# Four transformer layers with attention over a long context: where transposes, maxima and first products stand in the queues

## The chip, the cores and the metric

The kernel runs on one core of one Trainium2 chip. The metric is the device time of one execution in microseconds (us). TensorE (PE) multiplies, VectorE (DVE) reduces and does arithmetic, ScalarE (ACT) evaluates functions and copies, GpSimd (POOL) does small arithmetic and masks, SyncE (SP) issues DMAs. "PEld" is PE's weight load.

## The reference

`x` is 16 batch elements of 256 tokens by 128 channels, `ctx` 16 contexts of 1601 rows by 64 channels. Four layers follow each other, each an attention and a feed-forward part, each added to `x`:

```python
x = x + l0_attn(ln(x), ctx); x = x + l0_ffn(ln(x))   # self attention (causal) + cross attention, heads of 8
x = x + l1_attn(ln(x), ctx); x = x + l1_ffn(ln(x))   # cross attention, heads of 8
x = x + l2_attn(ln(x), ctx); x = x + l2_ffn(ln(x))   # self attention, then cross attention, heads of 32
x = x + l3_attn(ln(x), ctx); x = x + l3_ffn(ln(x))   # cross attention, heads of 8
# every attention: softmax(q k^T * scale) v, 16 heads; cross: k, v from ctx (1601 rows)
# the feed-forward parts: expert layers with top-k routing, and one quantised layer with a convolution
```

All of it is float32; the results are 16 x 256 x 128.

## The kernel before

**Units of work.** The cross attentions make up most of the work. There are 16 elements x 4 layers = 64 of them, and each is cut into four slabs of four heads (of 8 or of 32 channels), so 256 slabs: 192 with heads of 8 (`att.d8`), 64 with heads of 32. Two elements are under way at once (`LANES = 2`), and a list `seq` gives the order: for elements 0 and 1: l0 of both, l1 of both, l2 of both, l3 of both; then elements 2 and 3; eight rounds in all.

**A slab** goes through seven steps over its 13 tiles of 128 keys, two at a time. In a step PE makes transposed scores (`st_ops`, tile `st`), subtracting the maxima by further products with `nmT`; ACT takes the exponential (`exps`, L464, tile `p`); and PE multiplies the probabilities of the step before with the values (`weigh`, called from `weigh_back`), into an accumulator `av`, one bank of PSUM of 512 columns. With heads of 8, the values have a ninth column of ones, so that sums and values come out together (9 rows a head, columns 0 to 255 of the bank). With heads of 32, the values go to columns 0 to 255 (`av[:, 0, :]`) and the sums, products with `ones`, to columns 256 to 511 (`av[:, 1, :]`).

**Accumulators.** Before the first product, `zeroed` writes zeros over the accumulator with one product of a single row of zeros (`zero16`, a part of the tile `rows`): 256 columns for heads of 8, 512 for heads of 32. All other products add (`start` is False).

**Maxima.** While a slab is worked on, the maxima of the next one are prepared: 32 products per slab (`Slab.maxima`, tile `bank`), each reduced by DVE (L552, into `mx`), spread over steps 0 to 5. Then `Slab.thirds` reduces once more on DVE (L558, `nm`), and the helper `thirds` splits each maximum into three bfloat16 parts by four small POOL instructions (L509 to L512, tile `nmp`). Before, this is issued at the start of step 6. After the products of step 6 `Slab.shift` transposes `nmp` on PE, and ACT copies the result (`nmT`).

**The end of a slab.** The last products of a slab are issued in step 0 of the next one. `finish` then runs `normalised` as a generator: for heads of 8, ACT copies the accumulator (`y`, L488 calls the copy at L239), the generator yields, and when it is next advanced PE transposes `y` (L492), and DVE divides by the ninth column (L495, L496). For heads of 32 DVE does it all (L502, L503), without a yield. When the slab was the fourth, `att.done` is set, which lets the element's own chain go on.

**Slots.** All other work (layer norms, projections, feed-forward parts, self attention, loading and projecting the context) is written as generators. A slot (`slot()`) advances one of them after the other by one yield: first the pending `later` (the end of a slab), then one of two lines in turn (`key_line`, `value_line`, which make the keys and values), then each chain in the order of the list `chains`. After the products of each step come two slots, or three when the next entry of `seq` is an l2. The order of all instructions is fixed in this way when the program is built; every engine works off its own queue.

**Self attention** (`own_attention`, in l0 with heads of 8 and in l2 with heads of 32) runs inside slots: maxima for the four slabs (`mx`, L579), thirds, a shift of all four, and then per slot one slab's scores and exponentials, the next older one's sums (l2) and masks on POOL (`affine_select`, L603), and the values of the one before.

**DMAs around the change.** Queries and keys for heads of 8 are split into two parts (`hl`, L401 to L405, four buffers) and spread over partitions by SP (`spread`, L411): 16 DMAs for queries, 16 for an element's own keys, 4 for a slab of context keys. SP also loads the weights of the feed-forward parts (`stream`, L266, tile `ws`; `li` are those behind an l2 attention), which the kernel asks for three slots ahead of the product `down`, and the contexts (`cn`, L352 to L355), whose norms take POOL and DVE instructions over 128 x 832 elements (L361 to L370).

The lines that a generator resumes at are told by its yields. The matmul helper `mm` is L172; tiles tell its groups apart.

Of the kernel before, what the change touches and what calls it, by code (L numbers as in the profile page):

```python
# [20 lines left out]
P = 128  # L21
T = 256
# [52 lines left out]
def model(ctx: ExitStack, tc: tile.TileContext, d, out):  # L75
# [26 lines left out]
    ones = const.tile([P, P], F32, name="ones")  # L102
# [11 lines left out]
    zero16 = rows[0:1, : T // 2].bitcast(BF16)  # L114
# [56 lines left out]
    def mm(o, l, r, start=True, stop=True, free=False):  # L171
        nc.tensor.matmul(out=o, lhsT=l, rhs=r, start=start, stop=stop, skip_group_check=free)  # L172
# [6 lines left out]
    with setup as sp:  # L179
# [40 lines left out]
        for h0, c in ((64, 0), (96, P)):  # L220
            r = rows[h0 : h0 + 1, c : c + P]
# [14 lines left out]
    def evac(o, i, bias=None):  # L236

        if bias is None:
            nc.scalar.copy(o, i)  # L239
        else:  # L240
            nc.scalar.activation(o, i, AF.Identity, bias=bias)
# [222 lines left out]
        nc.scalar.activation(e[:r, :, :n, :], sc[:r, :, :n, :], AF.Exp, scale=att.scale)  # L464
        return e

    def zeroed(att):
        a = bank().rearrange("p (u q) -> p u q", u=2)
        n = 1 if att.d8 else 2
        mm(a[:, :n, :], zero16[:, :P], zero16.unsqueeze(1).broadcast_to([1, n, T]), True, False, True)  # L470
        return a

    def weigh(att, s, av, pr, t0, n, r, last, heads=range(4), sums=True, values=True):
        for i in range(n):
            fin = last and i == n - 1
            if values:
                for g in heads:
                    m = 9 if att.d8 else 32
                    mm(av[32 * g : 32 * g + m, 0, :], att.value(s, t0 + i, g, r), pr[g // 2][:r, g % 2, i, :],
                       False, fin, True)  # L480
            if sums and not att.d8:
                for g in heads:
                    mm(av[32 * g : 32 * g + 32, 1, :], ones[:r, :32], pr[g // 2][:r, g % 2, i, :], False, fin, True)

    def normalised(att, s, av):
        if att.d8:
            y = chan("y8")[:, :T]
            evac(y, av[:, 0, :])  # L488
            yield
            t = bank()  # L490
            for q in range(2):
                nc.tensor.transpose(t[:, q * P : (q + 1) * P], y[:, q * P : (q + 1) * P], ident)  # L492
            tv = t[:, :T].rearrange("p (q g e) -> p q g e", q=2, g=4)
            rc = sm.tile([P, 2, 4], F32, tag="rc8", name=name("rc8"))
            nc.vector.reciprocal(rc, tv[:, :, :, 8])  # L495
            nc.vector.tensor_tensor(  # L496
                att.o[:, :, 32 * s : 32 * s + 32].rearrange("p q (g e) -> p q g e", g=4),
                tv[:, :, :, :8], rc.unsqueeze(3).broadcast_to([P, 2, 4, 8]), ALU.mult,
            )
        else:  # L500
            rc = chan("rc")[:, :T]
            nc.vector.reciprocal(rc, av[:, 1, :])  # L502
            nc.vector.tensor_tensor(att.o[:, s, :], av[:, 0, :], rc, ALU.mult)  # L503
# [23 lines left out]
    class Slab:  # L527


        steps = [(t, min(2, NT - t), rows_of(t)) for t in range(0, NT, 2)]  # L530
# [13 lines left out]
        def maxima(self):  # L544

            g, q, c, k0, k1 = self.todo.popleft()
            att, s = self.att, self.s
            p = bank()
            h = slice(32 * g, 32 * g + 32)

            def reduce():
                nc.vector.tensor_reduce(self.mx[:, q, g, c : c + 1], p[:, : k1 - k0], AX.X, ALU.max)  # L552

            return lambda: mm(p[:, : k1 - k0], att.q[h, s, q * P : (q + 1) * P], att.k[s][h, k0:k1]), reduce
# [9 lines left out]
    def own_attention(att, causal, select):  # L564

        nm = sm.tile([P, 4, 2, 4], F32, tag="nm4", name=name("nm4"), bufs=1)
        for s in range(4):
            sc = [ps.tile([P, 2, 2, T], F32, tag="st", name=name("mx4")) for _ in range(2)]
            for q in range(2):
                for g in range(4):  # L570
                    h = slice(32 * g, 32 * g + 32)
                    mm(sc[g // 2][:, g % 2, q, :], att.q[h, s, q * P : (q + 1) * P], att.k[s][h, :],
                       q == 0, q == 1 and not causal)
            if causal:
                for g in range(4):
                    mm(sc[g // 2][:, g % 2, :, :], ident16, caus, False, True)
            for hp in range(2):
                o = nm[:, s, :, 2 * hp : 2 * hp + 2].rearrange("p q g -> p g q")
                nc.vector.tensor_reduce(o, sc[hp], AX.X, ALU.max, negate=True)  # L579
            yield  # L580
        for s in range(4):
            thirds(nmp[2 + s], nm[:, s, :, :])
            if s % 2:
                yield
        nmT = shift_T([nmp[2 + s] for s in range(4)])
        yield
        op, sign = select
        prs, avs, end = {}, {}, None
        for u in range(6):
            if end is not None:  # L590
                advance(end)
                end = None
            if 2 <= u:
                s = u - 2
                weigh(att, s, avs[s], prs.pop(s), 0, 2, P, True, sums=False)
                end = normalised(att, s, avs.pop(s))
                advance(end)
            if 1 <= u < 5:
                s = u - 1
                avs[s] = zeroed(att)  # L600
                weigh(att, s, avs[s], prs[s], 0, 2, P, True, values=False)
                for e in prs[s]:
                    nc.gpsimd.affine_select(  # L603
                        out=e, in_=e, pattern=[[0, 2], [sign * P, 2], [-sign, T]],
                        compare_op=op, fill=0.0, base=0, channel_multiplier=sign,
                    )
            if u < 4:
                prs[u] = [exps(att, t, 2, P) for t in st_ops(att, u, 0, 2, P, nmT[:, u, :])]
            yield
        advance(end)  # L610
        return att.o


# [442 lines left out]
    def advance(g):  # L1056
        try:
            return True, next(g)
        except StopIteration:
            return False, None  # L1060
# [62 lines left out]
    with tc.manual_schedule():  # L1123
        sl = slab(0)
        while sl.todo:
            for o in sl.maxima():
                o()
        sl.thirds()
        sl.shift()
        back = None  # L1130

        def weigh_back():

            nonlocal back
            if back is None:
                return
            sl, i, j, pr = back
            n = i // 4
            t0, m, r = sl.steps[j]
            if j == 0:  # L1140
                until(lambda: (0 if sl.att.d8 else sl.s) in v_of.get(n, {}))
                sl.att.v = v_of[n]
                sl.av = zeroed(sl.att)
            last = j == len(sl.steps) - 1
            weigh(sl.att, sl.s, sl.av, pr, t0, m, r, last)
            back = None
            if last:
                g = finish(sl, i)
                if advance(g)[0]:
                    later.append(g)  # L1150

        for i in range(4 * len(seq)):
            nxt = slab(i + 1)
            steps = sl.steps
            emitted = 0

            def maxima(want):

                nonlocal emitted
                ops = []  # L1160
                while nxt is not None and emitted < want:
                    a, c = nxt.maxima()
                    a()
                    ops.append(c)
                    emitted += 1
                for c in ops:
                    c()

            for j, (t0, m, r) in enumerate(steps):

                part = 32 * (j + 1) // (len(steps) - 1)
                if j < len(steps) - 1:
                    maxima(part - 3)
                elif nxt is not None:
                    nxt.thirds()
                sc = st_ops(sl.att, sl.s, t0, m, r, sl.nmT)
                pr = [exps(sl.att, t, m, r) for t in sc]
                if j < len(steps) - 1:
                    maxima(part)
                weigh_back()  # L1180
                back = (sl, i, j, pr)
                if j == len(steps) - 1 and nxt is not None:
                    nxt.shift()
                slot()
                slot()

                if i // 4 + 1 < len(seq) and seq[i // 4 + 1][1] == "l2":
                    slot()
            kp_room.give()
            sl = nxt  # L1190
        weigh_back()
        until(lambda: not chains and not later)

# [118 lines left out]
```

## Time and profile before

| | |
|---|---|
| median of 3 runs | 11116.24 us (11102.46 to 11129.85) |
| the profiled execution, its own time | 11069.08 us |
| its span, first to last instruction | 11067.1 us |
| mean granted PE clock | 0.815 |
| the zero product, 256 columns (heads of 8) | x256, 79.8 us busy, mean 312 ns |
| the zero product, 512 columns (heads of 32) | x128, 52.2 us busy, mean 408 ns |
| maxima, DVE (L552) | x8192, 4155.2 us busy, mean 567 ns |
| exponentials, ACT (L464) | x3840, 3500.5 us busy, mean 963 ns |
| thirds, POOL (L509 to L512) | x384 each, 83.6 + 78.9 + 83.6 + 89.2 us busy |
| masks, POOL (L603) | x256, 266.6 us busy, mean 1063 ns |

The profile is one execution. Busy time is the union of an engine's instructions; [...] In a list of waits, `PE bank L492 <- ACT y L239` means that PE, about to write `bank` at L492, was held until ACT had written `y` at L239; the numbers are the total, the count and the longest. In a timeline each row has the start, the length, the engine, the line, the operation and its tiles, and in brackets how long the engine had been idle before and what ended that. "PEclk" is the share of PE's clock that was granted.

### The profile page before, as it was taken

What the parts mean: (1) busy time and instruction counts of PE and PEld (TensorE: products, weight loads), DVE (VectorE), ACT (ScalarE), POOL (GpSimd) and SP (SyncE); (2) the same over time, 40 slices, a digit from 0 to 9 for tenths busy, and PEclk for the clock granted to TensorE, in tenths of its full rate; (3) what the DMA queues carried; (4) which work ended last, traced back from release to release, by engine and by line L of the source; (5) the groups of instructions that cost most, each with busy time, mean ns of one, the idle gap of its engine ahead of it and who ended that gap; (6) DMA issues with size and microseconds to landing.
All of it is one profiled execution on the core that took longest, in us unless ns stands there. A gap on an engine that the chain in (4) does not pass through costs nothing.

```text
span 11067.1 us, 204917 instructions
## 1 busy us (share of the span) xinstructions
PE 9761.1 (88%) x86834; PEld 5294.4 (48%) x86874; DVE 5929.3 (54%) x13070; ACT 4978.5 (45%) x6812; POOL 952.3 (9%) x2283
## 2 busy tenths in 40 slices
PE   6989899897998979889798897998979889898898
PEld 3445444454444544445454454444545445444454
DVE  5545555455554555545455454554555545465455
ACT  3544455444553445434454344543445434454444
POOL 2000100001000010000100001000010000100000
PEclk8779777797878978789777897778977789687898
DMA  2100111001110011100111001110011100111011
GB/s 58 37 7 15 36 45 37 7 16 39 42 37 7 19 38 42 34 7 19 38 44 32 7 19 42 40 32 7 19 38 43 33 7 19 38 44 32 7 24 27
DMA packets 158828, 313.10 MB, mean 28 GB/s; under 512 B 65163, under 2 KB 116275, under 8 KB 157910
## 3 DMA queue, kind: packets, MB, share of 16 engines
q1 hardware_dynamic: 154676, 297.83, 11.7%
q8 instruction: 683, 11.19, 0.4%
q14 instruction: 235, 1.93, 0.1%
q0 software_dynamic: 768, 1.48, 0.0%
q10 hardware_dynamic: 2466, 0.68, 0.0%
HBM read 98.31 MB, written 2.10 MB: 9 GB/s over the span
## 4 chain that ended last, share of the span: by engine, by line
PE 71%; DVE 14%; ACT 5%; issue 4%; POOL 3%; SPq 2%; DMA 1%; another core or an unknown queue 0%; DVEq 0%; POOLq 0%; ACTq 0%
PE bank L172 57%; PE st L172 10%; DVE mx L552 5%; ACT p L464 3%; DVE nm L579 2%; SPq L411 2%; PE mx L172 1%; PE bank L492 1%; POOL p L603 1%; PE bank L298 1%; DVE z L282 1%; POOL rs L278 1%; DVE st L275 1%; DVE hl L405 1%; ACT y L239 1%
## 5 line engine op out<-in xcount | busy, mean ns | idle before, releaser
L552 DVE TENSOR_REDUCE mx<-bank 128x1 f32<-128x400 f32 (+2 forms) x8192 | 4155.2, 567 | 2296.9 <-PE bank L172 2271.8
L464 ACT ACTIVATE p<-st 128x1024 f32<-128x1024 f32 (+1 forms) x3840 | 3500.5, 963 | 3568.3 <-PE st L172 2358.6
L172 PE MATMUL bank<-k,q 32*128 32x400 f32 (+2 forms) x10240 | 3573.1, 557 | 495.3 <-DVE mx L552 261.3
L172 PEld LDWEIGHTS bank<-k,q 32*128 32x128 f32 x10240 | 1600.6, 211 | 1928.7 <-DVE mx L552 1111.4
L172 PE MATMUL bank<-p,v 128*9 128x256 f32 (+3 forms) x27648 | 2412.4, 460 | 12.6 <-POOL p L603 12.6
L172 PE MATMUL st<-q,k 32*128 32x256 f32 (+1 forms) x18176 | 1974.8, 391 | 126.2 <-DVE nm L579 69.2
L172 PEld LDWEIGHTS st<-q,k 32*128 32x128 f32 (+1 forms) x18176 | 1300.8, 210 | 443.7 <-ACT p L464 140.4
L172 PE MATMUL st<-nmT,ones 32*128 32x512 bf16 (+1 forms) x7680 | 1270.1, 435 | 0.0
L172 PEld LDWEIGHTS bank<-p,v 128*9 128x9 f32 (+3 forms) x27648 | 676.3, 104 | 1175.4 <-issue 922.6
L172 PE MATMUL bank<-p,ones 128*32 128x256 f32 (+1 forms) x7680 | 607.1, 389 | 18.1 <-ACT p L464 18.1
L509 POOL CAST nmp<-nm 128x8 bf16<-128x8 f32 x384 | 83.6, 218 | 5441.9 <-DVE nm L558 3668.7
L278 POOL TENSOR_TENSOR rs<-rs,neghalf 128x2 f32<-128x2 f32 x240 | 167.5, 698 | 3491.1 <-DVE rs L277 3491.1
L172 PEld LDWEIGHTS <-ones 32*128 32x128 bf16 (+1 forms) x7680 | 408.1, 108 | 39.4
L579 DVE TENSOR_REDUCE nm<-mx 128x4 f32<-128x1024 f32 x256 | 301.8, 1221 | 215.3 <-PE mx L172 210.6
L239 ACT COPY v<-bank 128x512 f32<-128x512 f32 (+3 forms) x592 | 228.6, 448 | 328.8 <-PE bank L172 328.8
L172 PEld LDWEIGHTS bank<-p,ones 128*32 128x32 f32 (+1 forms) x7680 | 250.8, 113 | 216.6 <-ACT p L464 43.6
L502 DVE RECIPROCAL rc<-bank 128x256 f32<-128x256 f32 x128 | 224.9, 1757 | 193.6 <-PE bank L172 189.3
L603 POOL TENSOR_SCALAR_AFFINE_SELECT p<-p 128x1024 f32<-128x1024 f32 x256 | 266.6, 1063 | 653.3 <-PE bank L172 352.7
L464 ACT ACT_TABLE_LOAD x141 | 180.9, 1283 | 312.9 <-PE st L172 201.9
L172 PE MATMUL bank<-ws,h 128*128 128x128 f32 x1664 | 297.9, 343 | 3.2 <-DVE h L1027 0.8
L768 DVE TENSOR_TENSOR x<-bank,x 128x256 f32<-128x256 f32 x144 | 61.1, 425 | 446.0 <-PE bank L172 446.0
L172 PEld LDWEIGHTS bank<-ws,h 128*128 128x128 f32 x1664 | 267.2, 248 | 39.0 <-DVE mx L552 13.6
(240 smaller groups left out, 7274.4 us busy)
## 6 DMA issues: line engine op xcount, KB each, us to landing
k<-hl SPq DMA_DIRECT2D x768, 200.2 KB, 4.0
q<-hl SPq DMA_DIRECT2D x1024, 32.0 KB, 1.9
ws<-in_s_l_a_li_dram SPq DMA_DIRECT2D x32, 768.0 KB, 4.3
ws<-in_s_l3f_dram SPq DMA_DIRECT2D x32, 768.0 KB, 6.7
ws<-in_s_l0f_dram SPq DMA_DIRECT2D x32, 512.0 KB, 5.6
ws<-in_s_l_a_qkv_dram SPq DMA_DIRECT2D x16, 768.0 KB
k<-hl SPq DMA_DIRECT2D x256, 32.0 KB, 1.9
ws<-in_s_l3f_dram SPq DMA_DIRECT2D x16, 384.0 KB
```

The costliest lines, as they stand in the source:

```text
L172: nc.tensor.matmul(out=o, lhsT=l, rhs=r, start=start, stop=stop, skip_group_check=free)
L239: nc.scalar.copy(o, i)
L275: nc.vector.bn_stats(out=st[:, q, :], in_=src[:, q, :])
L278: nc.gpsimd.tensor_tensor(rs, rs, neghalf[:, 0:2], ALU.pow)
L282: nc.vector.tensor_scalar(z[:, q, :], src[:, q, :], mv[:, q, 0:1], rs[:, q : q + 1], ALU.subtract, ALU.mult)
L298: nc.tensor.transpose(p[:, q * P : (q + 1) * P], z[:, q, :], ident)
L411: nc.sync.dma_start(out=raw(o)[r::4, :], in_=raw(hl[c])[32 * s : 32 * s + 32, :])
L464: nc.scalar.activation(e[:r, :, :n, :], sc[:r, :, :n, :], AF.Exp, scale=att.scale)
L502: nc.vector.reciprocal(rc, av[:, 1, :])
L552: nc.vector.tensor_reduce(self.mx[:, q, g, c : c + 1], p[:, : k1 - k0], AX.X, ALU.max)
L579: nc.vector.tensor_reduce(o, sc[hp], AX.X, ALU.max, negate=True)
L603: nc.gpsimd.affine_select(out=e, in_=e, pattern=[[0, 2], [sign * P, 2], [-sign, T]], compare_op=op, fill=0.0, base=0, channel_multiplier=sign,
```

## The change

Four things are done:

1. `normalised` yields twice, not once, between the copy of `y` and its transposes. In `own_attention` the generator is advanced at the start of the next slot and then driven to its end after that slot's value products; at the end the rest takes a slot of its own.
2. `Slab.thirds` of the next slab is called in step 5, after the last maxima and ahead of `weigh_back` and the slots of that step, not at the start of step 6.
3. `zeroed` becomes `accumulators`: for heads of 32 nothing is written; the first product of each head into the bank has `start` set (the values in the cross attention; the sums in `own_attention`, where they come first and the values `after`). For heads of 8 the zero product stays.
4. The calls follow (`weigh` has a new argument).

```diff
-    def zeroed(att):
+    def accumulators(att):
+
         a = bank().rearrange("p (u q) -> p u q", u=2)
-        n = 1 if att.d8 else 2
-        mm(a[:, :n, :], zero16[:, :P], zero16.unsqueeze(1).broadcast_to([1, n, T]), True, False, True)
+        if att.d8:
+            mm(a[:, 0, :], zero16[:, :P], zero16, True, False, True)
         return a
 
-    def weigh(att, s, av, pr, t0, n, r, last, heads=range(4), sums=True, values=True):
+    def weigh(att, s, av, pr, t0, n, r, last, heads=range(4), sums=True, values=True, after=False):
+
         for i in range(n):
+            first = t0 + i == 0 and not att.d8
             fin = last and i == n - 1
             if values:
                 for g in heads:
                     m = 9 if att.d8 else 32
                     mm(av[32 * g : 32 * g + m, 0, :], att.value(s, t0 + i, g, r), pr[g // 2][:r, g % 2, i, :],
-                       False, fin, True)
+                       first and not after, fin, True)
             if sums and not att.d8:
                 for g in heads:
-                    mm(av[32 * g : 32 * g + 32, 1, :], ones[:r, :32], pr[g // 2][:r, g % 2, i, :], False, fin, True)
+                    mm(av[32 * g : 32 * g + 32, 1, :], ones[:r, :32], pr[g // 2][:r, g % 2, i, :],
+                       first and not values, fin, True)
 
     def normalised(att, s, av):
         if att.d8:
             y = chan("y8")[:, :T]
             evac(y, av[:, 0, :])
+            yield
             yield
             t = bank()
...
         for u in range(6):
-            if end is not None:
-                advance(end)
+            if end is not None and not advance(end)[0]:
                 end = None
             if 2 <= u:
                 s = u - 2
-                weigh(att, s, avs[s], prs.pop(s), 0, 2, P, True, sums=False)
+                weigh(att, s, avs[s], prs.pop(s), 0, 2, P, True, sums=False, after=True)
+                while end is not None and advance(end)[0]:
+                    pass
                 end = normalised(att, s, avs.pop(s))
                 advance(end)
...
             yield
-        advance(end)
+        while advance(end)[0]:
+            yield
         return att.o
...
                 if j < len(steps) - 1:
                     maxima(part - 3)
-                elif nxt is not None:
-                    nxt.thirds()
                 sc = st_ops(sl.att, sl.s, t0, m, r, sl.nmT)
                 pr = [exps(sl.att, t, m, r) for t in sc]
                 if j < len(steps) - 1:
                     maxima(part)
+                    if j == len(steps) - 2 and nxt is not None:
+                        nxt.thirds()
                 weigh_back()
```

More of the change, by code (lines that the diff above doesn't have):

```diff
@@ L599, in own_attention @@
                 s = u - 1
-                avs[s] = zeroed(att)
+                avs[s] = accumulators(att)
                 weigh(att, s, avs[s], prs[s], 0, 2, P, True, values=False)
@@ L1142, in weigh_back @@
                 sl.att.v = v_of[n]
-                sl.av = zeroed(sl.att)
+                sl.av = accumulators(sl.att)
             last = j == len(sl.steps) - 1
```

## The prediction

> **What bounds the kernel now.** I read the page first, then the list of waits of the matmul queue (PE), then the timeline around its longest waits, and beside them the order in which the instructions of the changed program stand on each engine.
>
> ```profile
> PE 9761.1 (88%) x86834; PEld 5294.4 (48%) x86874; DVE 5929.3 (54%) x13070; ACT 4978.5 (45%) x6812; POOL 952.3 (9%) x2283
> ...
> PE 71%; DVE 14%; ACT 5%; issue 4%; POOL 3%; SPq 2%; DMA 1%; another core or an unknown queue 0%; DVEq 0%; POOLq 0%; ACTq 0%
> ```
>
> Line 1 is busy time, line 2 the chain that ended last. PE bounds the kernel: a gain must come out of its work or its idle time (11067 - 9761 = 1306 us). The list of PE's waits says for whom it idled (total us, times, longest):
>
> ```profile
> PE bank L172 <- DVE mx L552: 261.3, 316, 5.4
> PE bank L492 <- ACT y L239: 144.1, 201, 2.4
> PE bank L172 <- POOL nmp L512: 136.3, 55, 6.4
> PE bank L172 <- DMA ws<-in_s_l_a_li_dram: 82.2, 7, 13.3
> ```
>
> Row 2 is the target of the first edit, row 3 of the second. Row 4 is not aimed at, but its DMAs change place. The timelines (start us, us, engine) show one case of each:
>
> ```profile
> 1788.32 0.62 PE L172 MATMUL bank<-p,v 65*9 65x256 f32 x8
> ...
> 1789.18 0.38 ACT L239 COPY y<-bank 128x256 f32<-128x256 f32 x1
> ...
> 1789.62 0.69 PE L492 MATMUL bank<-ident,y 128*128 128x128 f32 x2 [0.68 <-ACT y L239]
> ```
>
> The transpose stands right behind the products whose sums ACT must first copy.
>
> ```profile
> 2712.43 0.47 ACT L404 ACTIVATE hl<-bank,w_l_bcq 128x256 fp32r<-128x256 f32 x1 [3.97 <-DMA q<-hl]
> ...
> 2713.78 0.48 DVE L405 SCALAR_TENSOR_TENSOR hl<-bank,w_l_bcq,hl 128x256 fp32r<-128x256 f32 x1 [5.14 <-DMA q<-hl]
> 2714.18 0.18 DVE L558 TENSOR_REDUCE nm<-mx 128x8 f32<-128x32 f32 x1
> ...
> 2715.65 0.39 PE L172 MATMUL bank<-ident,nmp 128*128 128x128 bf16 x2 [5.80 <-POOL nmp L512]
> ```
>
> ```profile
> 1965.96 0.42 DVE L768 TENSOR_TENSOR x<-bank,x 128x256 f32<-128x256 f32 x1 [5.17 <-PE bank L172]
> ...
> 1976.23 0.60 DVE L282 TENSOR_SCALAR z<-x,mv,rs 128x128 f32<-128x128 f32 x2 [0.81 <-POOL rs L278]
> 1976.75 0.18 DVE L558 TENSOR_REDUCE nm<-mx 128x8 f32<-128x32 f32 x1
> ...
> 1978.21 0.39 PE L172 MATMUL bank<-ident,nmp 128*128 128x128 bf16 x2 [5.15 <-POOL nmp L512]
> 1978.39 0.63 PE L298 MATMUL bank<-ident,z 128*128 128x128 f32 x2
> ```
>
> PE waits for nmp because the small reduction nm stands in DVE's queue behind other work of the slots: a buffer that a DMA still reads (first case), or three chained layer norms (second). In the second case the next thing PE does is to transpose z, which those norms make.
>
> ```profile
> 2525.95 10.93 SPq L411 DMA_DIRECT2D q<-hl  x16
> ...
> 2536.98 13.17 SPq L411 DMA_DIRECT2D k<-hl  x20
> 2536.99 0.47 ACT L404 ACTIVATE hl<-bank,w_l_bcq 128x256 fp32r<-128x256 f32 x1 [6.59 <-DMA q<-hl]
> ...
> 2550.20 0.99 SPq L266 DMA_DIRECT2D ws<-in_s_l_a_li_dram  x1
> ...
> 2556.84 2.08 PE L172 MATMUL bank<-ws,oT 128*128 128x128 f32 x8 [11.43 <-DMA ws<-in_s_l_a_li_dram]
> ```
>
> SP issues a small DMA every 0.64 to 0.68 us; the weights that PE needs stand behind 36 of them.
>
> [...] here the mean granted clock is 0.815, and 0.93 in the dense stretch 700 to 1065 us against 0.75 from 1590 to 2110. [...]
>
> **The change part by part.** The program runs eight rounds of two batch elements; most stalls recur once a round.
>
> *Accumulators.* Of PE's 57277 products 128 go with their weight loads; [...] 64 stand in the model's own attention of layer l2. For 48 of them the starts of the trace's records are 0.31 us from last value product to zero and 0.32 from zero to first sum (mean of both together 0.70), against 0.20 where the two kinds meet directly: 48 x 0.5 = 24 us. The other 16 wait for the exponentials anyway: 0. The 64 of the cross attention mostly run beside a product of the maxima (start 0.03 us after it): 0.47 us against 0.42 without, 48 x 0.04, and some 0.2 for the other 16: 5 us. Sum 29; bounds 5 and 52 (the row's whole busy time, 128 x 408 ns).
>
> *Transposes.* 192 slabs have heads of 8. The step from last product to transpose is 1.07 us, against 0.31 when something unrelated follows: 0.76 each, 146 in all. But one slot on is not one stretch of PE work on: in the changed order nothing stands between in 138 of 192; 31 have four products of 256 columns (0.22 us apart, 0.86), 16 two key projections, 7 a set of maxima. 54 x 0.76 = 41 us. In the own attention of l0 the transposes now follow the next values; their waits were 5 us, of which I take 4. Sum 45, bounds 0 and 146 (no reason for a loss here: ACT's copy keeps its place). The slot moves att.done, and so the chains, on by one slot in steps; this is paid below.
>
> *Thirds.* nm and its four POOL instructions (0.22 us each) leave ahead of the slots of step 5. On DVE the norms, on POOL the selects of own attention (2.08 a pair) and powers come behind them, delayed by 0.2 and about 1.2 us, which the steps' PE work (about 6 us) hides; uncovered it would be 256 x 1.2 = 300 us. Four places hold 122 of the 143 us of such waits. (b) Behind a select in the first l2 layer, 1.97 a round: gone, 8 x 1.97 = 16. (a) and (c), behind the norms, 5.2 and 4.0 a round: the down product that feeds them now stands one slot later, behind step 5. From its end to z was 12.4 us; afterwards 3.5 us of PE work comes first, then the norms without the 3.0 us of maxima among them (about 9.1): 12.6. For (c) 12.2 becomes 13.6. What is late next is z: 8 x (0.2 + 1.4) = 13 us lost. (d) The stretch 2685 to 2716 with 15.4 us of waits: two context loads' norms hold POOL (5.40 and 2.94 on PE) and then hl holds DVE (5.80). In the new order one context load goes four slabs earlier and one behind it; hl's wait stays (12.0 us of SP issues less about 7.5 us of PE work: 4.3), and the early context norm (POOL 2.43 + 1.58, then two thirds of own attention, 1.9, against some 3 us of PE work) adds about 4 at its shift; with 1 for the rest: 15.4 - 9.3 = 6, less another for the second load, 5; 7 x 5 = 35. The many small waits, 21 us: 12 go.
>
> *SP.* Only the order changes. The query spread starts about 3 us earlier, but the li weights now stand behind 16 + 16 + 16 small DMAs, not 16 + 16 + 4. From 2523: 10.9, 10.3, 10.3 us end at 2554.5; li is then issued, and PE goes on 6.6 us later (as 2550.20 to 2556.84), at 2561.2 for 2556.8. 7 x 4.4 = 31 us lost. Bounds: 0 (the spread starts earlier still) and 10 a round.
>
> Sum: 29 + 45 + 16 - 13 + 35 + 12 - 31 = 93 us. The profiled execution took 11069.1 us (span 11067.1 and 2 around it), 47 below the median of the three runs; I take the 93 from the median: **11023 us**.
>
> **The rivals.** (1) *Waits only move.* Every stall of thirds and context returns at z, hl or the shift of own attention: 35 and 12 fall away, leaving 46, and a li wait at 10 us a round (70 for 31) leaves about 7: 11109. For it: two of four places already show the next late thing. Against: b, the zeros and the 54 transposes have nothing behind them. (2) *All waits go,* as the words of the change suggest: 146 + 143 + 29 = 318 less 31: 10829. Against it speak the 138 transposes with nothing ahead of them. A milder form: [...] at the chain's 71% on PE, 0.01 of clock is 0.01/0.815 x 0.71, about 95 us: 10930. (3) *Slower: SP.* The third spread ahead of li and of the context, and hl's wait now ahead of the exponentials of the next slab (in the program order the query split stands before them), so ACT, DVE and PE all stand until SP is through. Price: up to 10.3 us for the extra spread and 10.9 for the blocked stretch, twice a round. It decides when it takes over 124 us for the 31 counted, 18 us a round; at 24 a round, 168: 11160.
>
> **How the numbers follow.** Chances: forecast 0.50 (10975 to 11070), rival 1 0.20, rival 2 with its milder form 0.16, rival 3 0.14. No more than 2 in 10 lies outside 10900 to 11140: part of rival 2 and most of rival 3. 0.3% (33 us) is about what a measurement here can tell from no change. Faster: most of 0.50, 0.05 of rival 1, 0.16: 0.69; same 0.18; slower 0.13.
>
> **What would show it.** Right: no 128x512 zero product; waits of PE on ACT y near 100 us, not near 0; on nmp below 30; waits on z up by 40 or more; li still some 15 us in seven rounds; PE waits on DVE hl up. Wrong: y near zero (cover that I did not see), a li wait above 20 us a round (rival 3), or a clock off 0.815 by more than 0.01.

## The result, and the profile after

The changed kernel takes 11235.8 us (median of 4 runs, 11213.9 to 11250.3); the kernel before, run beside it, takes 11109.4 us (11066.2 to 11129.9). The ratio is **1.0117** (95% interval 1.0083 to 1.0152): 126 us slower, where 93 us faster was forecast. The profiled execution took 11250.3 us (span 11248.5), 181 more than the profiled one of before.

Busy time and the chain that ended last, of the changed kernel:

```profile
PE 9809.0 (87%) x86707; PEld 5327.0 (47%) x86746; DVE 5937.3 (53%) x13070; ACT 4977.0 (44%) x6812; POOL 953.1 (8%) x2283
...
PE 70%; DVE 12%; issue 7%; ACT 5%; POOL 2%; SPq 2%; DMA 1%; DVEq 0%; ACTq 0%; POOLq 0%
```

Of 181 us, 48 are longer busy time of PE (9809.0 for 9761.1, with fewer products) and 133 are idle time (1439.5 for 1306). The list of PE's waits of the changed kernel (total us, times, longest) says where:

```profile
PE bank L172 <- DVE mx L557: 354.5, 355, 6.0
PE bank L172 <- DVE hl L405: 159.0, 87, 9.8
PE bank L298 <- DVE z L282: 121.1, 21, 11.8
PE bank L497 <- ACT y L239: 107.9, 154, 1.8
...
PE bank L172 <- DMA ws<-in_s_l_a_li_dram: 54.2, 7, 8.4
...
PE bank L172 <- POOL nmp L517: 12.6, 15, 1.3
```

The aims were met: waits on nmp fell from 136 to 13 us, on y from 144 to 108, 160 us in all. Three others grew by more than that, 240 us: mx by 93, hl (L405) by 84, z by 62. The mx row is the one to look at, since no edit touches the maxima themselves. The longest of these waits recurs in every round in slabs 14 and 18 (counted from 0 in a round of 32, each from the shift of its own maxima to that of the next slab's), behind the second `down` product of an l2 part (the one whose sum is added to `x` at L966 before the change, L973 after it). The timeline of the kernel before at that place in round 2:

```profile
2080.59 0.42 DVE L966 TENSOR_TENSOR x<-bank,x 128x256 f32<-128x256 f32 x1 [11.35 <-PE bank L172]
...
2082.52 2.97 DVE L552 TENSOR_REDUCE mx<-bank 128x1 f32<-128x400 f32 x6
...
2085.41 0.59 DVE L282 TENSOR_SCALAR z<-x,mv,rs 128x128 f32<-128x128 f32 x2
...
2088.89 0.60 DVE L282 TENSOR_SCALAR z<-x,mv,rs 128x128 f32<-128x128 f32 x2 [0.82 <-POOL rs L278]
2089.29 0.73 PE L298 MATMUL bank<-ident,z 128*128 128x128 f32 x2 [2.66 <-DVE z L282]
```

And of the changed kernel:

```profile
2096.41 0.42 DVE L973 TENSOR_TENSOR x<-bank,x 128x256 f32<-128x256 f32 x1 [6.22 <-PE bank L172]
...
2099.25 0.60 DVE L282 TENSOR_SCALAR z<-x,mv,rs 128x128 f32<-128x128 f32 x2 [0.81 <-POOL rs L278]
...
2102.74 0.60 DVE L282 TENSOR_SCALAR z<-x,mv,rs 128x128 f32<-128x128 f32 x2 [0.82 <-POOL rs L278]
2103.26 2.50 DVE L557 TENSOR_REDUCE mx<-bank 128x1 f32<-128x402 f32 x5
2103.88 1.18 PE L172 MATMUL bank<-k,q 32*128 32x402 f32 x2 [5.98 <-DVE mx L557]
```

Before, the product came in the last slot of a step, so the six maxima of the next step (2.97 us) stood on DVE between the two norms that follow it. Now it comes one slot later, inside the next step: both norms stand in one piece (2096.4 to 2103.3) ahead of the five maxima, the banks fill, and PE waits 5.98 instead of 2.66 us. The first `down` product (slab 13, that of l1's feed-forward part, `w2q`, which is the prediction's second case) now stands between step 5 and the short step 6:

```profile
1980.08 2.05 PE L172 MATMUL bank<-w2q,h 128*128 128x128 f32 x16
...
1983.42 0.28 PE L172 MATMUL bank<-ident,nmp 128*128 128x128 bf16 x2
...
1990.86 0.73 PE L298 MATMUL bank<-ident,z 128*128 128x128 f32 x2 [7.15 <-DVE z L282]
```

The shift no longer waits, but PE waits for z: 7.15 us for the 5.15 on nmp. The queue of SP, with the product that waits for the li weights:

```profile
2558.69 10.03 SPq L411 DMA_DIRECT2D q<-hl  x16
...
2568.82 11.01 SPq L411 DMA_DIRECT2D k<-hl  x16
...
2579.92 10.10 SPq L411 DMA_DIRECT2D q<-hl  x16
2590.07 0.57 SPq L266 DMA_DIRECT2D ws<-in_s_l_a_li_dram  x1
...
2594.84 2.08 PE L172 MATMUL bank<-ws,oT 128*128 128x128 f32 x8 [8.27 <-DMA ws<-in_s_l_a_li_dram]
```

All three spreads stand ahead of li, as foreseen, yet PE waits less for li (8.27 for 11.43), as a wait on hl of 7.22 us now comes before it.

### The profile page after: what moved, and what is told of

Same layout as the page of the kernel before. It is cut to its first block, busy times and chain, and to the rows that moved or that the text cites. A ratio compares the mean times of both kernels' runs of the same rounds, so it can differ in the third digit from the quotient of the medians.

```text
span 11248.5 us, 204719 instructions
## 1 busy us (share of the span) xinstructions
PE 9809.0 (87%) x86707; PEld 5327.0 (47%) x86746; DVE 5937.3 (53%) x13070; ACT 4977.0 (44%) x6812; POOL 953.1 (8%) x2283
## 4 chain that ended last, share of the span: by engine, by line
PE 70%; DVE 12%; issue 7%; ACT 5%; POOL 2%; SPq 2%; DMA 1%; DVEq 0%; ACTq 0%; POOLq 0%
PE bank L172 56%; PE st L172 10%; DVE mx L557 4%; ACT p L464 3%; DVE nm L584 2%; SPq L411 2%; PE mx L172 1%; PE bank L497 1%; POOL rs L278 1%; PE bank L298 1%; DVE st L275 1%; POOL p L609 1%; DVE z L282 1%; DVE hl L405 1%; DVE mv L276 0%
## 5 line engine op out<-in xcount | busy, mean ns | idle before, releaser
L172 PE MATMUL bank<-p,v 128*9 128x256 f32 (+3 forms) x27648 | 2445.0, 464 | 33.2 <-POOL p L609 32.6
L172 PE MATMUL bank<-p,ones 128*32 128x256 f32 (+1 forms) x7680 | 641.3, 405 | 4.9 <-ACT p L464 4.6
L172 PEld LDWEIGHTS <-ones 32*128 32x128 bf16 (+1 forms) x7680 | 411.0, 108 | 34.2 <-issue 0.9
L172 PE MATMUL bank<-ws,h 128*128 128x128 f32 x1664 | 300.2, 345 | 15.2 <-DVE h L1034 12.5
```

## The experiments

**Theory A**: the loss is one of place (below also "phase"). The second yield sets `att.done` one slot later, each element's chain stands one slot later against the steps, and the DVE queue between steps changes as shown. **Rival B**: the early thirds, ahead of the norms on DVE and POOL, cost. Later theories are stated where they arise.

All runs in one table. Each ratio is to the kernel before on the same chip (its medians were 11081 to 11089 us). The last three columns are means over rounds 2 to 7 of one profiled execution each, worked out from the trace: length of a round, PE's idle time in it, and time lost to the clock, that is, half of the time at a granted clock of 0.5 (the records have only 0.5 and 1.0). The last two overlap where PE idles at the lower clock.

| kernel | ratio (95%) | round, us | idle | lost to clock |
|---|---|---|---|---|
| before | 1 | 1377.9 | 156.0 | 259.1 |
| changed | 1.0117 (1.0083, 1.0152) | 1399.5 | 174.1 | 263.4 |
| 1 thirds only | 0.9946 (0.9926, 0.9966) | 1369.9 | 146.6 | 251.7 |
| 2 edit 1 only | 1.0147 (1.0127, 1.0167) | 1401.2 | 174.6 | 261.1 |
| 3 chains a slot later only | 1.0324 (1.0304, 1.0344) | 1425.8 | 184.0 | 286.7 |
| 4 changed, chains in place | 0.9979 (0.9969, 0.9989) | 1376.7 | 140.4 | 271.9 |
| 5 edits 2 and 3 | 0.9941 (0.9921, 0.9961) | 1366.5 | 149.2 | 251.2 |
| 6 changed, l1 in place | 0.9915 (0.9897, 0.9932) | 1368.8 | 151.3 | 249.7 |
| 7 changed, l1 a step later | 0.9967 (0.9958, 0.9976) | 1376.7 | 162.1 | 244.9 |
| 8 as 4, two slots on | 0.9723 (0.9703, 0.9743) | 1343.1 | 139.0 | 227.8 |
| 9 as 8, last slab as 6 | 0.9715 (0.9694, 0.9735) | 1339.0 | 147.4 | 211.3 |
| 10 all two slots on | 0.9653 (0.9630, 0.9676) | 1332.4 | 149.4 | 207.4 |
| 11 before, one slot on | 1.0043 (1.0022, 1.0064) | 1384.0 | 149.2 | 271.6 |
| 12 before, two slots on | 0.9726 (0.9706, 0.9746) | 1340.9 | 147.6 | 215.6 |
| 13 before, products in the gap | 0.9870 (0.9850, 0.9891) | 1361.9 | 145.5 | 221.6 |
| 14 before, products elsewhere | 1.0227 (1.0205, 1.0248) | 1411.9 | 150.6 | 288.0 |
| 15 as 10, l1 in place | 0.9656 (0.9640, 0.9672) | 1328.9 | 142.2 | 207.4 |

**1. Thirds only.** The kernel before with edit 2 as in the diff above.

> Only edit 2: thirds one step earlier. Theory A (the loss is the slot that the second yield puts ahead of att.done, so that each element's chain stands one slot later against the steps): the thirds alone gain, ratio 0.990 to 0.998, waits on nmp below 40 us (136 before), no wait on z of 6 us or more. Rival B (the thirds themselves cost, by standing ahead of the norms on DVE and POOL): ratio 1.008 to 1.015, waits on z above 100 us as in the changed kernel (121).

0.9946: the thirds gain 60 us by themselves, so B falls. Waits on nmp are gone from the head of the list. Those on z rose from 58.7 to 109.3 us, over the 100 that B named:

```profile
PE bank L298 <- DVE z L282: 109.3, 41, 12.2
```

So the early thirds do make z late, but the kernel gains all the same. (The longest wait on z, which A wanted below 6 us, was 11.8 us before the change already.)

**2. Edit 1 only.** `normalised`'s second yield and the new order in `own_attention`.

> Only edit 1: the second yield and what goes with it in own attention. Theory A: slower, ratio 1.010 to 1.020 (the changed kernel's 1.012 and what the other two edits give), with waits of PE on DVE mx near 350 us and one of about 6 us at the second down product of each l2 part. Rival B: ratio 0.993 to 1.000, since the transposes only gain cover.

1.0147. Edit 1 alone carries the whole loss, and the waits on mx with it:

```profile
PE bank L172 <- DVE mx L553: 353.0, 357, 6.0
```

**3. Chains a slot later only.** The transposes stay where they were:

```diff
         while not att.done:
             yield
+        if att.d8:
+            yield
...
         advance(end)
+        if att.d8:
+            yield
         return att.o
```

> The kernel before with one idle yield after an attention with heads of 8 is done, so that the chains stand one slot later as in the changed kernel; transposes, thirds and zero products stay where they were. Theory A: slower, ratio 1.012 to 1.022, a little above the run with edit 1 alone, as the transposes gain no cover. Rival B: within 0.3% of the kernel before.

1.0324, more than A asked: one idle yield behind each attention with heads of 8 (two in l0, one in l1 and in l3), with the same instructions, costs 359 us. Idle time grows by 28.0 us a round, loss to the clock by 27.6.

```profile
PE bank L172 <- DVE mx L552: 376.7, 379, 6.0
```

Run 2 has the chains in the same place and moves the transposes besides. It is 200 us faster than run 3 (11250 and 11450 us on one chip), with 25.6 us a round less lost to the clock. Behind late chains the moved transposes gain; runs 4 and 11 show what they do where the chains keep their place.

**4. Changed, chains in place.**

```diff
             yield
-            yield
+            if s < 3:
+                yield
             t = bank()
```

> The changed kernel, but the second yield only for the first three slabs of four, so that att.done is set in the slot of before and the chains keep their place. Three in four transposes stay one slot on, thirds and accumulators stay as changed. Theory A: faster than the kernel before, ratio 0.985 to 0.995, waits on mx back near 260 us. Rival B: still slower, ratio 1.008 to 1.013. If a third cause (the start flags of the accumulators) is at work: slower too.

0.9979: the loss is gone and the waits on mx are back where they were, as A has it, though the ratio falls short of the 0.985 to 0.995 that A asked.

```profile
PE bank L172 <- DVE mx L558: 255.4, 284, 5.4
```

The run is not even as fast as the thirds alone, although PE idles 6.2 us a round less: its granted clock is 0.803 against 0.817. So a second question stands: what do moved transposes do to the clock?

**5. Edits 2 and 3, no yield.**

> Edits 2 and 3 without edit 1: thirds one step earlier and the accumulators without zero products; every transpose stands where it stood before. Beside the run with the yield on three slabs of four (0.998, granted clock 0.803) it tells what keeps that one behind the thirds alone (0.995, 0.817). Theory T (moving the transposes lowers the granted clock and so gives back what it saves in idle time): ratio 0.990 to 0.994, clock 0.815 or more. Rival S (the accumulators' start flags, or the missing zero products, cost): ratio about 0.998, clock near 0.803.

0.9941. S falls: the accumulators don't cost; against run 1 they gain 0.05% at intervals of 0.2% on either side, too little to tell. Moving three in four transposes one slot on (and edit 1's order in own attention) is what separates run 4 from this one, 10.2 us a round: idle 8.8 us less, lost to the clock 20.7 more.

**6. Changed, l1 in place.** As in run 4, but for l1's attentions alone (`if not (att.l1 and s == 3): yield`).

> The changed kernel, with the second yield left out for the last slab of the l1 attentions alone: l1's att.done, and with it the way through l1's feed-forward and l2's own attention, keeps its old slot; all else is as changed. In the changed kernel slabs 12 to 19 of a round are about 34 us longer than in the run with the yield on three slabs of four. Theory A (phase of the chain): that comes back, 8 x 34 = 270 us, ratio 0.985 to 0.995. Rival (the loss is spread over all layers): a third of it, ratio 1.005 to 1.010.

0.9915, as A has it: the whole loss sat in l1's chain. The second `down` product has maxima between its norms again; first the list of waits, then the timeline of this run:

```profile
PE bank L172 <- DVE mx L559: 257.0, 344, 2.9
PE bank L172 <- DVE hl L405: 164.9, 87, 9.3
```

```profile
2060.96 0.42 DVE L976 TENSOR_TENSOR x<-bank,x 128x256 f32<-128x256 f32 x1 [10.97 <-PE bank L172]
...
2062.89 2.97 DVE L559 TENSOR_REDUCE mx<-bank 128x1 f32<-128x400 f32 x6
...
2069.66 0.73 PE L298 MATMUL bank<-ident,z 128*128 128x128 f32 x2 [2.92 <-DVE z L282]
```

In slabs 12 to 19 of a round the changed kernel is 34.8 us longer than this run; 20.7 of them are idle time of PE. Of these, 17.4 lie in slabs 13, 14, 17 and 18, where the two products shown stand (13 and 14 for one element, 17 and 18 for the other), and 2.7 in slab 16, in a further wait on mx. The waits on hl stay at 165 us in this fast kernel, so they are not what made the changed one slow.

**7. Changed, l1 a whole step later.** Two idle yields after an l1 attention, three slots in all.

> The changed kernel with two more idle yields after an l1 attention is done: there a step has three slots, so l1's chain stands three slots, one whole step, later than before. Theory A1 (what counts is the place within the step: a down product in the step's last slot has the next maxima between its two norms on DVE, elsewhere the two norms run together ahead of them): about as fast as the run with l1 in its old place, within 0.5% of it, and no wait on mx of 5 us at the second down product. Rival A2 (later is worse in itself): slower than the changed kernel, ratio 1.015 or more.

0.9967, between the two and 0.52% from run 6, just outside what A1 said; A2 falls. At the second `down` product PE waits 2.67 and 2.55 us for z, as A1 has it. At the first it waits 6.85 and 4.37 for mx. In run 6 the six maxima of step 5 (2.97 us) stand between the first norm's statistics and its z. A step later the next step is step 6, which has no maxima, so the three norms run in one piece (1961.9 to 1970.7) and five maxima of the slab after wait behind them. A whole step on restores the place within a step, but not which step it is.

**8. Two slots on for three slabs of four.** As run 4, with two further yields where `s < 3` in place of one.

> The changed kernel, but two more yields for the first three slabs of four and none for the last: three in four transposes stand behind a whole step's products, and the chains keep their place. The waits on ACT y fall to about a quarter of 144 us or less. If idle time alone counts (the record's second rival in small): some 60 us below the run with one yield on three slabs of four, ratio 0.989 to 0.993. Theory T (denser placing is given back through the clock): ratio 0.996 or more, clock 0.803 or less.

0.9723, better than either side said: theory T falls, and idle time alone is not what counts. Waits on y fall to 34.2, idle time stays (139.0 for 140.4), and the gain is in the clock: 0.834.

**9. Two slots on, last slab as in run 6.**

```diff
             yield
-            yield
+            for _ in range(2 if s < 3 else 0 if att.l1 else 1):
+                yield
...
```

The part left out sets `att.l1` for the l1 attentions, as in runs 6 and 15.

> The version that the runs so far point to: transposes two slots on for the first three slabs of four; the last slab's one slot on in l0 and l3, and in place in l1. If the two gains add (two slots for one: 0.9723 against 0.9979; l1 alone in place against all in place: 0.9915 against 0.9979): ratio 0.963 to 0.968. If both come through the same granted clock and overlap: 0.970 to 0.974.

0.9715, the same as run 8 within the intervals: the gains overlap.

**10. All two slots on.** Three yields for every slab, and one idle yield after an l1 attention, so that all chains stand one step later.

> The changed kernel with two more yields for every slab and one idle yield after an l1 attention: every chain stands one whole step later than before (two slots where a step has two, three where it has three). Theory A1 (place within the step): near the run whose chains keep their place with two slots for the others (0.9723), the last quarter of the transposes gains besides and the first down product in l2 loses (as it did when l1 alone stood a step later, 0.5%): ratio 0.967 to 0.978. Rival A2 (later is worse): 0.985 or more.

**0.9653**, 10701 us, a little better than A1 said; with run 15 the fastest kernel found. PE is busy for 9459.9 us only (9761.1 before), at a clock of 0.847, and waits for y once in the whole execution:

```profile
PE bank L498 <- ACT y L239: 0.5, 1, 0.5
```

**11 and 12. The transposes alone,** on the kernel before, three slabs of four, one slot on and two slots on, with edit 1's order in own attention; chains, thirds and zero products as before.

> The kernel before, with the transposes of the first three slabs of four one slot on and nothing else: the prediction's term for the transposes by itself, without the phase. The prediction's term: three quarters of 45 us, ratio 0.996 to 0.998, waits on ACT y near 105. What the run with thirds and accumulators showed (0.9979 against 0.9941 without the move): idle time gained, clock lost, ratio 1.000 to 1.006, granted clock 0.805 or less.

> The kernel before, with the transposes of the first three slabs of four two slots on and nothing else. If the gain of two slots is the transposes' own: ratio 0.974 to 0.982, granted clock 0.830 or more. If it needs the early thirds beside it: 0.985 to 0.993, clock near 0.815.

1.0043 and 0.9726. Run 11 is the prediction's term for the transposes by itself. One slot on, waits on y fell to 95.4 us and idle time by 6.8 us a round, somewhat more than was worked out, yet the kernel loses. Two slots on, PE idles about as long (147.6 for 149.2), but the round is 43 us shorter. Spans and granted clocks of the two profiled executions:

```profile
core 0: 11122.0 us, clock 0.806
```

```profile
core 0: 10787.1 us, clock 0.839
```

One slab (number 11 of round 2) in the kernel before, in run 11 and in run 12, as an example (its means over rounds 2 to 7 are 28.3, 32.1 and 25.4 us); columns are the stretch, its length, busy time of the engines, granted clock, DMA share and GB/s:

```profile
1893.00:1920.00 27.00, 24.64 (x236) 10.82 (x235) 17.00 (x35) 16.56 (x24) 0.88 (x4) 0.94 0.31 87
```

```profile
1894.00:1926.00 32.00, 30.39 (x247) 13.52 (x249) 17.09 (x35) 17.12 (x26) 0.87 (x4) 0.73 0.28 74
```

```profile
1842.00:1867.00 25.00, 23.41 (x247) 10.72 (x239) 17.10 (x35) 16.89 (x25) 0.88 (x4) 1.00 0.32 93
```

DVE and ACT do the same work in nearly the same busy time in all three. PE has 247 products in run 11 and in run 12, but is busy for 30.39 us at a clock of 0.73 and for 23.41 us at 1.00.

**13 and 14. Is it activity?** Theory H, a guess that these two runs test: the wait on y (144.1 us in 201 waits before) falls around the short step 6, and low activity of PE there sets off drops of the clock. If so, useless work in just that gap should speed the kernel up.

```diff
             yield
             t = bank()
+            for q in range(2):
+                mm(t[:, q * P : (q + 1) * P], ident, ident)
             for q in range(2):
                 nc.tensor.transpose(...)
```

Run 14 puts the same two products behind the value products of step 3, into a bank of their own.

> The kernel before with two products more ahead of every pair of transposes of y (256 times): the identity by itself, 128x128 in float32, into the bank that the transposes then overwrite, so that PE is busy while ACT copies y. The result is unchanged. Theory H (the halved clock is set off by low activity around the short step 6, where the wait on y lies, and activity there keeps the clock up): despite 512 more products of about 0.3 us the time is the same or shorter, ratio 0.975 to 1.000, granted clock 0.825 or more. Rival G (the clock follows the order of work in another way): the products cost what the wait does not hide, ratio 1.000 to 1.008, clock 0.81 to 0.82.

> Control for the run with products in the gap: the same two products, 192 times, behind the value products in the middle of a slab (step 3), where PE has no gap. About 192 x 0.65 us at full clock, 125 us more work: ratio 1.008 to 1.014 if activity counts only where it is low; below 1.003 if more activity anywhere raises the clock by as much as it costs.

0.9870: with 512 products more, the kernel is 1.3% faster. The group of these products (each has two records) and the wait of run 13:

```profile
L172 PE MATMUL bank<-ident 128*128 128x128 f32 x1024 | 213.7, 340 | 1.6 <-ACT h L1021 1.6
```

```profile
PE bank L494 <- ACT y L239: 11.8, 25, 1.2
```

The useless products are busy for 213.7 us, and the whole of PE is busy 43 us less than before (9717.7), at a clock of 0.840. Run 14 is slower than either side said (1.0227, clock 0.799): its 384 products are busy for 189.6 us, and the kernel takes 254 us more. They also take a bank of their own, which those of run 13 don't, so that the two runs differ in more than the place; this was not taken apart. H holds for the gap: with products there the clock is 0.840, for 0.815 before. It does not explain run 14. Stretches at the halved clock that begin within 5 us behind a transpose of y (a coincidence in time, not a proof for each): 101 before, 85 in run 11, 32 in run 12, 21 in run 13. Why one slot on is worse than none is not settled by this: run 11 has fewer such stretches than the kernel before, and 334 elsewhere for 303.

**15. All two slots on, l1 in place.**

```diff
             yield
-            yield
+            for _ in range(0 if att.l1 and s == 3 else 2):
+                yield
...
```

> The version with two more yields for every slab, but l1's last transposes in their old place (no yield more, and none after the attention), so that l0 and l3 stand one whole step later and l1's chain where it was. In the run with all two slots on, slabs 12 to 18 of a round came to about 4 us a round more than in the run whose chains keep their place. Theory A: 8 x 4 = 35 us below it, ratio 0.960 to 0.965. Rival (the gains overlap): 0.965 to 0.969.

0.9656, the same as run 10, as the rival said: once the transposes are covered, moving l1's chain by a whole step costs nothing that could be measured, although PE waits on mx for 400.1 us in run 10 and for 288.7 here.

## Why the prediction was wrong, step by step

- **The failed step is the phase**, that is, the price of the chains' later place. The prediction said: "The slot moves att.done, and so the chains, on by one slot in steps; this is paid below." What it paid was 13 us at z and 31 at li. Run 3 puts the price of that slot alone at 359 us; beside the other edits, the changed kernel against run 4, it is 1.4% (1.0117 for 0.9979), some 150 us. The prediction looked only at the places where PE waited on nmp. The second `down` product, where nothing was to be removed, was not looked at: 5.98 and 5.19 us on mx now stand where 2.66 and 2.54 on z stood, 6.0 a round or 48 us. At the first one PE waits for z 2.0 us longer than it had waited for nmp, for each of the two elements (7.15 for 5.15, 5.93 for 3.98; 3.9 a round, 32 us), where 0.2 and 1.4 had been taken. More is lost to the clock around these stalls: in slabs 16 to 18, 17.3 us a round in the changed kernel against 0.6 in run 6 (both above run 5; these times overlap with idle). Over the whole round that loss grew by 4.3 us only (263.4 for 259.1), so the result of the change itself is mostly idle time (18.1 us a round).
- **The term for the transposes had the wrong sign where the chains keep their place.** Forecast for three quarters of 45 us: a gain of 34. Alone they cost 0.43%, 48 us (run 11). The idle part was right in kind, 8 x 6.8 = 54 us; what failed is that only idle time was priced. Lost to the clock: 8 x 12.5 = 100 us more. Behind the later chains the whole move gains 200 us (run 2 against run 3), so the two terms don't add, and neither is a fixed price.
- **The price of the clock was right, and not used.** The prediction had 95 us for 0.01 of granted clock, as a mild form of rival 2. Between runs 11 and 12, at equal idle time, the clock is 0.806 and 0.839 in the profiled executions, whose spans are 11122.0 and 10787.1: 101 us for 0.01. It was kept for a rival that only gains.
- **Thirds**: forecast in sum 16 - 13 + 35 + 12 = 50 us gained before SP; run 1 measured 0.54%, 60 us. Waits on z rose by 51 in that run (40 or more was foreseen). Of the 35 at the context loads little came: PE's idle time in slabs 27 and 28 fell by 2.7 us a round in run 1, about 20 us, but their length by 0.9 only. That the sum came near is in part luck.
- **SP**: forecast 31 us lost at li. The order is as foreseen, and the waits on li fell from 82.2 to 54.2 us, since hl takes the time first (both together rose by 56). Rival 3, the one that ended slower, describes this wait on hl rightly (74.6 to 159.0 us), but it is not the cause: run 6 keeps it and is 0.85% faster than the kernel before. The sign of that rival came true by another mechanism.
- **Accumulators**: 29 us forecast; run 5 against run 1 shows 0.05%, within the uncertainty. That a first product with `start` set costs nothing of its own was an assumption of the forecast; it was not measured apart from this. No zero product of 512 columns is left.
- **What would show it**: y near 100 (107.9), nmp below 30 (12.6), z up by 40 or more (62), hl up and no zero product of 512 columns all came; the wait on li, 7.7 us a round for the 15 named, did not. None of the three signs of being wrong came either (y near zero, li above 20 us a round, a clock off 0.815 by more than 0.01: it was 0.813). So the signs only showed that the aimed-at waits had moved. The list had no row for a wait on mx, the one that grew most.
- **Rival 1**, "waits only move", was nearer in kind: waits came back at z and hl as it says. But it too had no wait on mx, and it stopped at a gain of 7 us.
- **Rival 2**, "all waits go", was turned down as 138 transposes had nothing ahead of them. With two slots the wait on y does go, and 0.9653 is 385 us, more than its 287. But most of that is clock: a round has only 6.6 us less idle time than before, and loses 51.7 us less to the clock.

## What to carry to other kernels

A yield more in a generator moves everything behind it: before pricing what it covers, list what the later chain meets in each queue, at every place and not only at those with a stall today. A gap on PE cost more than its idle time here (run 13: 213.7 us of useless products in it, and the kernel 1.3% faster); where the granted clock swings, look at the clock of the stage beside its idle time, and try a move by two slots as well as by one. In these runs a transpose that waits for a copy stood better two slots on, behind the next step's products (0.9726), than one slot on (1.0043).

## What the runs showed of the hardware that was not expected

- Useless products in a gap made the kernel faster (run 13, 0.9870, at a clock of 0.840 for 0.815 before), and 384 of the same ones in a dense place cost about twice what was expected: 254 us measured, at a clock of 0.799, against an estimate of 125 (192 pairs of 0.65 us at full clock; a pair of run 13, at 1708.76 us in a stretch at clock 1.00, took 0.71). Why the dense place loses clock is open.
- At nearly equal idle time of PE (149.2 and 147.6 us a round), moving two instructions by one more slot, in three slabs of four with heads of 8, was worth 3.2% (1.0043 and 0.9726): the round is 43.1 us shorter, and 56.0 us less of it is lost to the clock (271.6 and 215.6). Why one slot on is worse than none is open.
- The trace of the kernel before has the clock at 1.0 or 0.5 only, in stretches of 3.41 us and multiples of it (all but one of 808). 404 of them are at 0.5, 4088 us in all, and 146 of these are 3.41 us long. Cut into windows of that length, the trace has PE busy for 94% of a window at 1.0 on average where the next one is at 1.0 too, and for 66% where the next one is at 0.5. A single long stall did not have to come first: of the 404 stretches, 41 begin in a wait of PE of over 3 us or within two windows behind it.
